# Skip term D·u moved from TensorE to VectorE, paired x-projections, and earlier copies of turned exponentials in a Mamba–attention–feed-forward kernel

## The chip, the core and the metric

The kernel runs on one core of one Trainium2 chip. The metric is device time in microseconds (us). Three runs before the change gave 4987.43, 4989.93 and 4991.37 us; the median is 4989.93 us. One further execution was recorded by the hardware profiler: it took 4984.05 us, of which the program's span in the trace is 4982.3 us, so 1.75 us lie around the span.

The engines are named as in the profile: PE is TensorE's matmul side and PEld its weight loads, DVE is VectorE, ACT is ScalarE, POOL is GpSimd, SP is SyncE, which here only issues transfers. Each engine takes its instructions in one order that is fixed when the program is built.

## What is computed

Eight images of 384 channels and 32x32 pixels (1024 tokens) go through two layers, all in fp32. The first is a convolution beside a bidirectional selective scan (Mamba); the second is causal self-attention with six heads of 64 and a group-quantised feed-forward net, both with residuals. Cut to what the change touches:

```python
# mamba, called forward and on the flipped sequence; the two are added
x_dbl = einsum('blc,ec->ble', u, x_proj_w)              # 24 + 16 + 16 rows
dt, Bm, Cm = split(x_dbl, ...)
delta = softplus(einsum('blr,dr->bld', dt, dt_proj_w) + dt_proj_b)
h = exp(delta * A) * h + (delta * u) * B                # per step, 16 states
y = sum_n h * C
y = (y + u * D_param) * silu(z)                         # the skip term D u
# attention
attn = softmax(where(causal, q @ k.T, -inf)); out = attn @ v
```

## The kernel before, in words

Channels lie on partitions: 384 channels are three groups `c` of 128, and 1024 tokens are two halves `h` of 512, so that nearly every tile is 128x512 fp32, which is also one PSUM bank.

**Stages.** `before_scan` (L307) prepares one image: norm, input projection, causal convolution in both directions `d`, gates, the x-projection to delta, B and C (`project`, L484), and `delta` (L511). The scan is cut into units: one image, one channel group, one of four parts (direction and half, in the order `PARTS`), and two of the 16 states. A unit goes through `slot` (its steps are spread over consecutive slots): loads, `s_first` (POOL: delta·u times B, L588), `s_scan` (ACT: exp into a `da` bank, L601; DVE: the scan, L606; POOL: times C, L612), `s_sum` (PE: eight transposing matmuls add the unit into the `y` bank, L620; at the end of a run y is copied out by ACT at L636 or added by DVE at L641), and `s_gate` (L643), which runs once per image, channel group and half, 48 times in all. `attention` (L676) follows image by image, and `feed_forward` (L970) for the first five images.

**Order of work.** `run` and the timed list at the end of the kernel lay the scan slots of later images beside attention, feed-forward and preparation of others. That is only the order in which instructions are traced. The framework's scheduler then fixes each engine's own order from a priority that follows the traced order and from its own estimate of when operands are ready. `tc.high_priority(offset=n)` moves what is traced inside it forward by n in that priority. `pin` (L73) keeps an instruction behind the one traced just before it on its engine.

**Buffers.** PSUM has eight banks: y 1, da 2, s 2, pt 2, av 1. A scan unit's `g` tile has six buffers. The banks of tag `pt` are shared by the transposes of attention, by the row factors `f`, by parts of `before_scan`, and by `s_gate`.

**s_gate.** The tile `us` holds u of both directions added, `sz` the gate silu(z). Before the change PE put D·u into a `pt` bank with one matmul against a diagonal matrix `diagd` (L656; built at L181 to L183), added eight transposes of the two `yt` tiles on top (L661), and DVE multiplied the gate by the bank (L670). A matmul of fp32 that isn't a transpose appears as two instructions in the profile, so these 48 are 96 there.

**project.** For each image, channel group and half one bank `xp` is filled by two matmuls of 64 columns, one for each direction, on partitions 0 to 63 and 64 to 127 (L487). ACT or DVE then reads the bank.

**turned and weigh.** In attention, `scores` (L774) leaves exponentials `pr` in SBUF (DVE L802, ACT L812). `turned` (L858) transposes blocks of them on PE into a `pt` bank (L864), and ACT copies the bank to SBUF as `ptn` (L866, 576 copies; two buffers for each head of a pair). `weigh` (L869) multiplies the values by `ptn` (L877), one block behind. `at_once(second)` is a local helper in `attention`: it wraps the second matmul of a pair in `tc.high_priority(offset=HURRY)` with HURRY = 400, and is used at L788 and L877 together with `pin`.

Of the kernel before, what the change touches and what calls it, by code (L numbers as in the profile page):

```python
# [12 lines left out]
ALU = mybir.AluOpType  # L13
# [41 lines left out]
def kernel(  # L55
# [49 lines left out]
    def half(h):  # L105
        return slice(h * HB, (h + 1) * HB)
# [71 lines left out]
    amat = ctile("amat", [P, NC, NS])  # L178
    nc.scalar.activation(amat, vec[:, :, V_ALOG : V_ALOG + NS], AF.Exp)
    nc.vector.tensor_scalar(amat, amat, -1.0, None, ALU.mult)  # L180
    diagd = ctile("diagd", [P, NC, P])  # L181
    for c in range(NC):
        nc.vector.tensor_scalar(diagd[:, c, :], ident, vec[:, c, V_D : V_D + 1], None, ALU.mult)  # L183
    rssm = ctile("rssm", [P, 1])
    nc.vector.tensor_tensor(rssm, sc[:, 0:1], sc[:, 1:2], ALU.mult)
    rsh = ctile("rsh", [P, 1])
# [9 lines left out]
    def binarize(src, dst, nk, nout, per, name, emit):  # L196

        gs = nout // GROUPS
        st = {}

        def part(w, k, n):
            return w[k * P : (k + n) * P, :].rearrange("(k p) e -> p k e", p=P)

        def view(k, n):
            t = btile(f"{name}_{k}")
            v = t.rearrange("p c l -> p (c l)")[:, : n * nout].rearrange("p (k e) -> p k e", k=n)
            nc.scalar.dma_start(out=v, in_=part(src, k, n))
            return v

        starts = list(range(0, nk, per))  # L210

        @emit
        def _():
            st["mps"] = bank(f"mps_{name}", "av")

        for k in starts:

            @emit
            def _(k=k, n=min(per, nk - k)):
                v = view(k, n)  # L220
                sums = small.tile([P, GROUPS], F32, name=f"sums_{name}_{k}", tag="bsums", bufs=1)
                for g in range(GROUPS):
                    nc.vector.tensor_reduce(
                        sums[:, g : g + 1], v[:, :, g * gs : (g + 1) * gs], AX.XY, ALU.add
                    )
                nc.tensor.matmul(
                    out=st["mps"][:, :GROUPS],
                    lhsT=onesc,
                    rhs=sums,
                    start=(k == 0),  # L230
                    stop=(k == starts[-1]),
                )

        @emit
        def _():
            st["mean"] = small.tile([P, GROUPS], F32, name=f"mean_{name}", tag="bmean", bufs=1)
            nc.vector.tensor_scalar(
                st["mean"], st["mps"][:, :GROUPS], C / (gs * nk * P), None, ALU.mult
            )

        for k in starts:

            @emit
            def _(k=k, n=min(per, nk - k)):
                v = view(k, n)
                for g in range(GROUPS):
                    z = v[:, :, g * gs : (g + 1) * gs]
                    nc.vector.tensor_scalar(z, z, st["mean"][:, g : g + 1], None, ALU.subtract)
                t = btile(f"sg_{name}_{k}")
                sg = t.rearrange("p c l -> p (c l)")[:, : n * nout].rearrange("p (k e) -> p k e", k=n)  # L250
                z, sg = v[:, :, : GROUPS * gs], sg[:, :, : GROUPS * gs]
                nc.scalar.activation(sg, z, AF.Sign)
                nc.vector.tensor_tensor(sg, sg, z, ALU.subtract)
                nc.vector.tensor_tensor(z, z, sg, ALU.add)
                nc.vector.memset(v[:, :, GROUPS * gs :], 0.0)
                nc.scalar.dma_start(out=part(dst, k, n), in_=v)


    def mean_of(c_of, name):
# [47 lines left out]
    def before_scan(b, tags, emit, later=None, diags=None):  # L307
# [107 lines left out]
        for c in range(NC):  # L415

            @emit
            def _(c=c):
                st["up", c] = mtile(f"up_{b}_{c}")
                for d in range(2):  # L420
                    st["u", d, c] = mtile(f"u{d}_{b}_{c}")
                if c + 1 < NC:
                    weights_of(c + 1)

            for i, to in enumerate((emit, emit if later is None else later)):
                for h in range(NH):
                    to(lambda c=c, i=i, h=h: in_proj(c, i, h), 2.6)
            for d in range(2):
                for h in range(NH):
                    emit(lambda c=c, d=d, h=h: conv(c, d, h), 3.0)  # L430

            def silus(ts):
                for t in ts:
                    pin(nc.scalar.activation(t, t, AF.Silu))

            def sum_of_us(c=c):
                usum = mtile(f"us_{b}_{c}")
                nc.vector.tensor_tensor(usum, st["u", 0, c], st["u", 1, c], ALU.add)
                spill((b, "us", c), usum, f"sus_{b}_{c}")
                for d in range(2):  # L440
                    spill((b, "u", d, c), st["u", d, c], f"su_{d}_{b}_{c}")


            def gates(c=c, silus=silus, sum_of_us=sum_of_us):
                st["xc"] = mtile(f"xc_{b}_{c}")
                load(st["xc"], x[b, chunk(c), :])
                accs = [local(c, h) for h in range(NH)]
                with tc.high_priority(offset=60):
                    us = [st["u", 0, c], st["u", 1, c]] if later is None else []
                    silus(us + [st["z", c]])  # L450
                    for h in range(NH):
                        pin(
                            nc.scalar.activation(
                                accs[h], accs[h], AF.Tanh, scale=0.5, bias=dwbh[:, c : c + 1]
                            )
                        )
                    pin(nc.scalar.preload_act_table_set(LOG_EXP))
                for h in range(NH):
                    acc, xc = accs[h], st["xc"][:, half(h)]
                    nc.vector.scalar_tensor_tensor(  # L460
                        acc, acc, 1.0, st["xn"][:, c, half(h)], ALU.add, ALU.mult
                    )
                    nc.vector.scalar_tensor_tensor(xc, acc, rsh, xc, ALU.mult, ALU.add)  # L463
                spill((b, "t", c), st["xc"], f"st_{b}_{c}")
                spill((b, "z", c), st["z", c], f"sz_{b}_{c}")
                if later is None:
                    sum_of_us()

            def gates_of_us(c=c, silus=silus, sum_of_us=sum_of_us):
                with tc.high_priority(offset=60):  # L470
                    silus([st["u", 0, c], st["u", 1, c]])
                    pin(nc.scalar.preload_act_table_set(LOG_EXP))
                sum_of_us()

            if later is None:
                emit(gates, 14.0)
            else:
                emit(gates_of_us, 4.0)
                later(gates, 10.0)


            for h in range(NH):

                def project(c=c, h=h):  # L484
                    xp = bank_of(f"xp_{b}_{c}_{h}")
                    for d in range(2):
                        nc.tensor.matmul(  # L487
                            out=xp[d * DW : (d + 1) * DW, :],
                            lhsT=wx[:, c, :],
                            rhs=st["u", d, c][:, half(h)],  # L490
                            start=True,
                            stop=True,
                        )
                    xd = st["xd"][:, half(h)]
                    if c == 0:
                        nc.scalar.activation(xd, xp, AF.Identity, bias=onerow)
                    else:
                        nc.vector.tensor_tensor(xd, xd, xp, ALU.add)

                emit(project)  # L500
# [142 lines left out]
    def s_gate(u):  # L643
# [6 lines left out]
        for what in ("us", "z"):  # L650
# [2 lines left out]
            both.append(t)  # L653
        us, sz = both
        tp = bank(f"yb_{u.name}", "pt")
        nc.tensor.matmul(  # L656
            out=tp, lhsT=diagd[:, c, :], rhs=us, start=True, stop=False, skip_group_check=True
        )
        for yt in yts:
            for i in range(QT):  # L660
                nc.tensor.matmul(  # L661
# [1 line left out]
                    lhsT=yt[:, i, :],  # L663
                    rhs=ident,
                    is_transpose=True,
                    start=False,
                    stop=(yt is yts[-1] and i == QT - 1),
                    skip_group_check=True,
                )
        nc.vector.tensor_tensor(sz, sz, tp, ALU.mult)  # L670
        t = dram.tile([P, HB], F32, name=f"sgy_{u.name}", tag=f"sp_gy_{c}_{h}")
        nc.sync.dma_start(out=t, in_=sz)
# [3 lines left out]
    def attention(b, emit_ffn, emit):  # L676
# [79 lines left out]
            st["o"] = btile(f"o_{b}")  # L756

        def at_once(second):  # L760
            return tc.high_priority(offset=HURRY) if second else nullcontext()

        def rows_of(e):
            return slice(e * HD, (e + 1) * HD)
# [57 lines left out]
        def weighted_values(c, g, steps):  # L822
# [35 lines left out]
            def turned(j):  # L858
                cols = slice(max(j - g * QT, 0) * P, HB)
                for e in range(2):  # L860
# [2 lines left out]
                        pr = st["pr", c, g, i, j // QT]  # L863
                        nc.tensor.transpose(pt[:, chunk(i)], pr[:, e, chunk(j % QT)], ident)  # L864
                    ptn = ptp.tile([P, HB], F32, name=f"ptn_{b}_{c}_{g}_{j}_{e}", tag=f"ptn{e}")
                    nc.scalar.copy(ptn[:, cols], pt[:, cols])  # L866
                    st["ptn", j, e] = ptn

            def weigh(j):  # L869
# [354 lines left out]
```

## Time and profile before

| quantity | value |
|---|---|
| median of three runs | 4989.93 us |
| profiled execution | 4984.05 us |
| its span | 4982.3 us |
| mean granted TensorE clock | 0.884 of full speed |
| HBM traffic | 527.33 MB read, 165.68 MB written, 139 GB/s |
| transfers on SP's queue | 40.9% of the 16 DMA engines' time |
| scan transposes L620 | 6144 instructions, 949.1 us busy on PE |
| state multiplications L588 and L612 | 768 each, 1840.4 and 1822.1 us busy on POOL |
| scans L606 | 1536, 906.5 + 953.3 us busy on DVE |
| exponentials L601 | 1536, 1057.3 us busy on ACT |

A line of the profile's groups reads: source line, engine, operation, what is written from what, shape, count; then busy time and the mean duration of one in ns; then how long the engine had been idle just before such instructions, and what ended that idle time. Busy time is a union: two matmuls that overlap count once. Matmul ends are modelled in the trace, so busy PE time is not work at peak rate.

The scan ends at about 4680 us, and image 7's attention follows it without scan work beside it.

### The profile page before, as it was taken

Reading aid. Unit: us, or ns where it says so; the run is one execution under the profiler, and the core shown is the slowest. Engines: PE = TensorE matmul, PEld = TensorE weight load, DVE = VectorE, ACT = ScalarE, POOL = GpSimd, SP = SyncE. Lnnn points to the kernel's source line nnn. Section 1 sums busy time; section 2 is a strip of 40 time slices with the busy share of each in tenths; the row PEclk is TensorE's granted clock in tenths of the full one; section 3 lists DMA queues with packets and bytes.
Section 4 is the critical chain, followed back from the end, with each engine's and each line's share of the span. In section 5 each row is a group of like instructions: output and inputs, shape, how many; then the busy total and the mean of one; then the engine's idle time right before and its main releaser. Section 6 shows DMA issues by size and latency. Waiting matters only on the chain. (4 is left out here: it accounts for less than half of the span.)

```text
span 4982.3 us, 50788 instructions
## 1 busy us (share of the span) xinstructions
PE 4058.8 (81%) x16458; PEld 2192.3 (44%) x16458; DVE 3607.8 (72%) x4771; ACT 2668.1 (54%) x4858; POOL 3696.0 (74%) x1944
## 2 busy tenths in 40 slices
PE   3687786988888888788787888887888988888989
PEld 1243343544444444345443444443454544444444
DVE  6887988677886768786778867687867676676623
ACT  4575655565554655545656446555456365464425
POOL 0578687997768986779876788867789888888800
PEclk7788797899989899888998888998899988999999
DMA  6554646324463335463334633334533333334210
GB/s 230 204 185 151 200 164 229 114 93 130 140 220 120 112 116 168 136 200 123 100 125 147 210 111 129 112 130 157 193 130 116 113 110 124 131 102 137 93 58 26
DMA packets 365010, 696.36 MB, mean 140 GB/s; under 512 B 30104, under 2 KB 88904, under 8 KB 364744
## 3 DMA queue, kind: packets, MB, share of 16 engines
q1 hardware_dynamic: 355232, 676.97, 40.9%
q10 hardware_dynamic: 9512, 16.15, 0.9%
q8 instruction: 130, 2.13, 0.2%
q14 instruction: 136, 1.11, 0.1%
HBM read 527.33 MB, written 165.68 MB: 139 GB/s over the span
## 5 line engine op out<-in xcount | busy, mean ns | idle before, releaser
L588 POOL TENSOR_TENSOR g<-ud,bc 128x1024 f32<-128x1024 f32 x768 | 1840.4, 2396 | 579.8 <-PE y L620 452.0
L612 POOL TENSOR_TENSOR g<-g,bc 128x1024 f32<-128x1024 f32 x768 | 1822.1, 2373 | 251.7 <-DVE g L606 157.8
L601 ACT ACTIVATE da<-dl,amat 128x512 f32<-128x512 f32 x1536 | 1057.3, 691 | 1532.5 <-DVE g L606 1498.3
L606 DVE TENSOR_TENSOR_SCAN g<-da,g 128x512 f32<-128x512 f32 x768 | 906.5, 1210 | 475.4 <-POOL g L588 457.2
L606 DVE TENSOR_TENSOR_SCAN g<-da,carry,g 128x512 f32<-128x512 f32 x768 | 953.3, 1271 | 384.2 <-POOL g L588 354.1
L620 PE MATMUL y<-ident,g 128*128 128x128 f32 x6144 | 949.1, 303 | 266.7 <-POOL g L612 123.1
L620 PEld LDWEIGHTS y<-ident,g 128*128 128x128 f32 x6144 | 789.3, 156 | 714.4 <-issue 418.9
L788 PE MATMUL s<-k,q 64*128 64x512 f32 (+3 forms) x1152 | 384.5, 600 | 128.9 <-DVE nm L802 110.5
L802 DVE CUSTOM_DVE_ANT_0 pr<-s,cmask 128x512 f32<-128x512 f32 (+3 forms) x576 | 299.5, 545 | 178.2 <-PE s L788 177.9
L812 ACT ACTIVATE pr<-pr,nm 128x512 f32<-128x512 f32 (+3 forms) x576 | 348.9, 607 | 123.5 <-DVE nm L802 121.6
L864 PE MATMUL pt<-ident,pr 128*128 128x128 f32 x1728 | 304.0, 309 | 93.6 <-ACT ptn L866 55.1
L995 PE MATMUL hp<-t,w 128*128 128x512 f32 x720 | 334.9, 610 | 28.7 <-DMA w<-w1s 18.3
L1039 PE MATMUL yp<-h,w 128*128 128x512 f32 x720 | 332.6, 620 | 15.3 <-DMA w<-w2s 12.1
L864 PEld LDWEIGHTS pt<-ident,pr 128*128 128x128 f32 x1728 | 217.7, 155 | 245.0 <-ACT ptn L866 110.3
L877 PE MATMUL av<-ptn,v 128*64 128x512 f32 (+3 forms) x1152 | 273.1, 555 | 50.4 <-ACT ptn L866 33.9
L341 PE MATMUL in<-xn,win 128*128 128x512 f32 x576 | 282.3, 636 | 32.3 <-DVE xc L463 8.6
L866 ACT COPY ptn<-pt 128x512 f32<-128x512 f32 (+3 forms) x576 | 255.3, 472 | 49.8 <-PE pt L864 48.4
L727 PE MATMUL qp<-t,wqk 128*128 128x512 f32 x576 | 266.4, 613 | 11.7 <-DVE t L302 9.1
L400 DVE SCALAR_TENSOR_TENSOR loc<-xn,vec,loc 128x496 f32<-128x496 f32 (+3 forms) x384 | 259.9, 721 | 19.5 <-ACT loc L389 18.2
L788 PEld LDWEIGHTS s<-k,q 64*128 64x128 f32 x1152 | 132.3, 206 | 261.2 <-DVE nm L802 179.6
L611 POOL COPY carry<-g 128x2 f32<-128x2 f32 x384 | 87.0, 226 | 205.9 <-DVE g L606 205.8
L1039 PEld LDWEIGHTS yp<-h,w 128*128 128x128 f32 x720 | 142.0, 201 | 189.1 <-issue 169.4
(153 smaller groups left out, 4722.4 us busy)
## 6 DMA issues: line engine op xcount, KB each, us to landing
bc<-rows SPq DMA_DIRECT2D x512, 512.0 KB, 4.1
dl<-sdl SPq DMA_DIRECT2D x160, 256.0 KB, 2.9
ud<-sud SPq DMA_DIRECT2D x160, 256.0 KB, 2.7
t<-st SPq DMA_DIRECT2D x63, 512.0 KB, 5.1
su<-u SPq DMA_DIRECT2D x48, 512.0 KB, 3.4
du<-su SPq DMA_DIRECT2D x96, 256.0 KB, 3.8
sdl<-du SPq DMA_DIRECT2D x96, 256.0 KB, 2.8
sud<-du SPq DMA_DIRECT2D x96, 256.0 KB, 2.3
```

The costliest lines, as they stand in the source:

```text
L341: nc.tensor.matmul(out=mp, lhsT=st["win", c][:, k, i, :], rhs=st["xn"][:, k, half(h)], start=(k == 0), stop=(k == NC - 1),)
L588: pin(nc.gpsimd.tensor_tensor(g, ud, sst["bc", 0, u.b, u.part, u.n], ALU.mult))
L601: nc.scalar.activation(da, sst["dl", u.b, u.c, u.part], AF.Exp, scale=amat[:, u.c, n : n + 1])
L606: nc.vector.tensor_tensor_scan(gi[:, ::step], da[:, ::step], gi[:, ::step], first, ALU.mult, ALU.add)
L612: pin(nc.gpsimd.tensor_tensor(g, g, sst["bc", 1, u.b, u.part, u.n], ALU.mult))
L620: nc.tensor.matmul(out=y[:, j, :], lhsT=g[:, i, chunk(j)], rhs=ident, is_transpose=True, start=(u.opens and i == 0 and j == 0), stop=(u.cl ...
L788: mm = nc.tensor.matmul(out=ss[e][:, : k1 - k0], lhsT=st["q"][rows_of(e), c, chunk(qi)], rhs=st["k"][rows_of(e), c, k0:k1], start=True, st ...
L802: nc.vector.tensor_tensor_reduce(out=x, in0=ss[e][:, :w], in1=mask, scale=-1.0, scalar=-MASKED, op0=ALU.add, op1=ALU.min, accum_out=m,)
L812: nc.scalar.activation(x, x, AF.Exp, bias=m, scale=-1.0, accum_out=rs[:, i, e, kb : kb + 1])
L864: nc.tensor.transpose(pt[:, chunk(i)], pr[:, e, chunk(j % QT)], ident)
L995: nc.tensor.matmul(out=hp, lhsT=st["w1"][:, c, chunk(m % 2)], rhs=st["xn"][:, c, half(h)], start=(c == 0), stop=(c == NC - 1),)
L1039: nc.tensor.matmul(out=yp, lhsT=st["w2", k // 6][:, k % 6, :], rhs=st["h", k // NC][:, k % NC, half(h)], start=(k == 0), stop=(k == NF - 1),)
```

## The change

Three edits, and one that only moves a helper.

1. The diagonal matrices and the diagonal matmul of `s_gate` are gone. The first transposing matmul of each gate opens the bank. DVE then adds D·u to the bank in place with one `scalar_tensor_tensor` (u times a per-partition scalar, plus the bank), ahead of the multiplication by the gate.
2. The second direction's x-projection is traced at priority offset 400 and pinned behind the first's.
3. The copies `ptn` are traced at priority offset 60.

`at_once` moves from `attention` to the kernel's outer scope, so that `project` can use it too.

```diff
-    diagd = ctile("diagd", [P, NC, P])
-    for c in range(NC):
-        nc.vector.tensor_scalar(diagd[:, c, :], ident, vec[:, c, V_D : V_D + 1], None, ALU.mult)
...
+    def at_once(second):
+
+        return tc.high_priority(offset=HURRY) if second else nullcontext()
...
                     for d in range(2):
-                        nc.tensor.matmul(
-                            out=xp[d * DW : (d + 1) * DW, :],
-                            lhsT=wx[:, c, :],
-                            rhs=st["u", d, c][:, half(h)],
-                            start=True,
-                            stop=True,
-                        )
+                        with at_once(d == 1):
+                            mm = nc.tensor.matmul(
+                                out=xp[d * DW : (d + 1) * DW, :],
+                                lhsT=wx[:, c, :],
+                                rhs=st["u", d, c][:, half(h)],
+                                start=True,
+                                stop=True,
+                            )
+                        if d == 1:
+                            pin(mm)
...
         tp = bank(f"yb_{u.name}", "pt")
-        nc.tensor.matmul(
-            out=tp, lhsT=diagd[:, c, :], rhs=us, start=True, stop=False, skip_group_check=True
-        )
         for yt in yts:
             for i in range(QT):
                 nc.tensor.matmul(
...
                     is_transpose=True,
-                    start=False,
+                    start=(yt is yts[0] and i == 0),
                     stop=(yt is yts[-1] and i == QT - 1),
                     skip_group_check=True,
                 )
+        nc.vector.scalar_tensor_tensor(tp, us, vec[:, c, V_D : V_D + 1], tp, ALU.mult, ALU.add)
         nc.vector.tensor_tensor(sz, sz, tp, ALU.mult)
...
-                    nc.scalar.copy(ptn[:, cols], pt[:, cols])
+                    with tc.high_priority(offset=60):
+                        nc.scalar.copy(ptn[:, cols], pt[:, cols])
```

More of the change, by code (lines that the diff above doesn't have):

```diff
@@ L756, in _ @@
             st["o"] = btile(f"o_{b}")
-        def at_once(second):
-            return tc.high_priority(offset=HURRY) if second else nullcontext()
         def rows_of(e):
```

## The prediction, made before the changed kernel had run

> **What bounds the kernel now.** I read the page's first two parts first, then the list of waits, then the rows of the lines that the diff touches.
>
> ```profile
> PE 4058.8 (81%) x16458; PEld 2192.3 (44%) x16458; DVE 3607.8 (72%) x4771; ACT 2668.1 (54%) x4858; POOL 3696.0 (74%) x1944
> PE   3687786988888888788787888887888988888989
> POOL 0578687997768986779876788867789888888800
> PEclk7788797899989899888998888998899988999999
> ```
>
> No engine is full. PE is nearest, at eight tenths in most slices and alone in the last two, and POOL stands beside it from the third slice to the 38th. The clock row matters as much: where PE has gaps it is granted less than full speed. So PE's idle time is the place to look: 4982.3 - 4058.8 = 923.5 us. The waits of all engines, longest first (engine and line, releaser, total us, times, longest):
>
> ```profile
> ACT da L601 <- DVE g L606: 1498.3, 1071, 14.7
> DVE g L606 <- POOL g L588: 811.3, 448, 10.2
> POOL g L588 <- PE y L620: 452.0, 202, 14.1
> ...
> PE y L620 <- POOL g L612: 123.1, 51, 10.5
> ```
>
> Read backwards, this is a ring: exponentials wait for scans, scans for POOL, POOL for PE to free a g buffer (452.0 us), and PE for POOL (123.1 us). POOL waits for PE over three times as long as PE for POOL. I take PE's ordered queue, its work and its small stalls, as what mostly sets the pace, with POOL close behind. The waits of PE alone:
>
> ```profile
> PE s L788 <- DVE nm L802: 110.5, 89, 3.4
> PE y L620 <- ACT yt L636: 77.0, 22, 11.9
> PE y L620 <- DVE yt L641: 56.2, 17, 7.5
> PE pt L864 <- ACT ptn L866: 55.1, 43, 3.8
> ...
> PE av L877 <- ACT ptn L866: 33.9, 16, 4.0
> ...
> PE pt L864 <- DVE zh L670: 22.5, 11, 3.5
> ...
> PE f L849 <- ACT ptn L866: 14.3, 11, 3.5
> ```
>
> The copies ptn end 55.1 + 33.9 + 14.3 us here and 1.8 at L656, 105.1 us of PE's idle time, in 73 waits; the gate's product zh ends 22.5 us of it. The groups' rows of the matmuls that go or are paired:
>
> ```profile
> L656 PE MATMUL yb<-ush,diagd 128*128 128x512 f32 x96 | 60.0, 712 | 3.7 <-ACT ptn L866 1.8 <-DVE du L527 1.1 <-ACT u L379 0.5
> L487 PE MATMUL xp<-u,wx 128*64 128x512 f32 x192 | 78.2, 704 | 60.5 <-ACT u L434 49.9 <-ACT u L379 9.8 <-DVE zh L670 0.9
> ```
>
> **What the Trainium skill says.** "TensorE: Matmul & The Clock Gate", Part 1, says that the array runs at full or half rate by how busy it has been of late. The trace agrees: L656 takes 592 ns at least and 1222 at most, and PEclk averages 0.884. So a PE with less to do may be granted less. The same page (section on the array's architecture) says that ACT and DVE keep strict FIFO order; so a copy moved forward can also hold up what stands behind it. Nothing in this trace contradicts that. "TensorEngine Tiling (Array Packing)", Key Properties, says that tiles run in parallel, and 64 columns make two tiles. The trace shows it at L487, on PE's timeline with start, duration and count: the four instructions of two directions take 1.08 us, those of one direction at both halves 1.93.
>
> ```profile
> 1242.73 1.08 PE L487 MATMUL xp<-u,wx 128*64 128x512 f32 x4
> ...
> 471.76 1.93 PE L487 MATMUL xp<-u,wx 128*64 128x512 f32 x4
> ```
>
> "VectorE: DVE Perf Modes", the tier table, puts any two-tensor operation that reads PSUM at one element a cycle. The row below has the same form as the new addition (SBUF times a per-partition scalar, plus PSUM, into PSUM), so its duration is used.
>
> ```profile
> L369 DVE SCALAR_TENSOR_TENSOR u<-up,vec,u 128x512 f32<-128x512 f32 x90 | 66.0, 745 | 3.4 <-ACT u L358 3.3
> ```
>
> **The change, part by part.** Beside the trace I compared the order of instructions in the two built programs, engine by engine. POOL's is identical, 1949 of 1949. On PE 144 instructions give way to 96 (the 48 diagonal matmuls go, the 96 projections have a new line), on DVE 48 additions come and three diagonal builds go. SP issues the same 1724, most in the same order. ACT's order changes most.
>
> *Diagonal matmul.* One matmul is two instructions. In a dense stream one takes 0.43 us (24 of L1039 in 10.30 us, in the chain of waits), so one matmul 0.86 us, as PE's starts around L656 show where the clock is full. 48 x 0.86 = 41 us at full speed, 41 / 0.884 = 47 us as granted; 60.0 us is the row's busy time, with the pipeline's filling, and is the upper bound. What reaches the end depends on PE's next stall. Following PE's records from each of the 48 to the next gap over 0.3 us, the gap is ended by something other than a scan sum in 33 cases (attention's own transposes, scores, projections: these come earlier too when PE does) and in 15 by L620, where PE waits for POOL or for the y copy and simply waits longer. 47 x 33/48 = 32 us. Bounds: 15 (a third) to 60.
>
> *Copies ptn.* Matching each copy with its transposes by order, copies start on average 1.1 us after their last transpose ended (sum 635 us over 576), mostly because ACT is in exponentials pr (L812) or da (L601). In the new order 335 of the 375 displaced copies stand earlier; together they pass 218 pr and 144 da. With L812 at 607 + 188 ns (the row of the accumulator read) and L601 at 691 ns: 218 x 0.795 + 144 x 0.691 = 273 us over 576 copies, 0.47 us each. 73 stalls x 0.47 = 34 us of PE idle time. Half of it will meet the next stall (scores waiting for nm, 110.5 us, are in the same stretches): 17 us gained. The exponentials that are passed are covered: an exp da takes 0.69 us and a scan 1.21 to 1.27, with two da banks, so ACT has 0.5 us a scan to spare, and DVE waits for da only 42.4 us now (L606's two rows, 27.5 + 14.9). Bounds: -10 (copies that block ACT) to 60 gained.
>
> *Paired projections.* The tie holds nothing back: it brings the second direction forward only once it can run, and the first is issued as before. In the order, 31 of 48 pairs stand side by side before, 33 after; three are won and one is lost. Saved: 2 x (1.93 - 1.08) = 2 us. Bounds 0 to 5.
>
> *The new addition.* 48 x 0.745 = 36 us more on DVE, which is 72% busy, so most of it lies in DVE's idle time. What reaches PE: the pt bank comes free 0.745 us later after the last transpose. PE waited for zh in 14 cases on its list (11 at L864, three elsewhere): 14 x 0.745 = 10 us lost. The bank is opened 0.86 us later, so the hold as a whole isn't longer. Scans queue behind the additions on DVE: the 36 us meet POOL's product L612, which waited 157.8 us for scans; I take a tenth, 3 us. Bounds 3 to 36. What hides the rest is DVE's wait for POOL (811.3 us).
>
> *The rest.* The transfers of us and z wait for the same DVE instructions; one table load of 1.28 us less on ACT, two copies of v on DVE instead of ACT: nothing.
>
> Sum: -32 - 17 - 2 + 13 = -38 us against the profiled execution, 4984.05 - 38 = 4946 us. The median of the runs stands 5.9 us above that execution, so 4989.93 - 38 = 4952 us.
>
> **Rivals.** *A: PE's gain turns into waiting.* Stalls at L620 (123.1 + 77.0 + 56.2 = 256 us) grow by what PE saves while POOL, at 6 to 9 tenths in the later half, sets the pace. For: POOL's row. Against: POOL's 452.0 us behind PE. Then the final stage and a few stretches gain: about a quarter of 51 us less the 13 us of DVE: nothing, 4990 us.
>
> *B: slower. ACT is blocked by the earlier copies.* A copy that stands ahead of da but whose transposes are late holds the queue. ACT already idles 48.4 us for pt before copies (62 times), and about 120 of the 576 copies start within 0.15 us of their transposes, so they have no room to come earlier. If 200 copies hold ACT for 0.47 us, that is 94 us; when over half of that appears in scans waiting for da, 47 + 13 us of loss stand against 32 + 2 us of PE's gain, the copies' own gain being gone: 26 us more, 5016 us. Against: only 144 exponentials da are passed, and ACT is 46% idle.
>
> *C: the copies were the lever.* Nearly all the 105.1 us go, and the denser PE keeps its clock: -32 - 60 - 2 + 10 = -84, 4906 us. For: they are late by 635 us in sum. Against: only 273 us of passing.
>
> **How the numbers follow.** Forecast 0.55 (4920 to 4978), A 0.2, B 0.17, C 0.08. Below 0.2%, 10 us, a difference can't be told from none here. Faster: the forecast, C and 0.07 of A: 0.70. Same: 0.12 of A and 0.01 of B: 0.13. Slower: 0.17, most of B and a rest of A. The range 4905 to 5008 leaves out about half of C's and half of B's chance and the forecast's tails, under 0.2; it is set by the unknown pass-through (15 to 60) and the copies (-10 to 60).
>
> **What would show it.** Right: no L656; PE busy lower by 45 to 60 us; a new DVE row of 48 at about 745 ns; waits of L864, L877 and L849 for ptn down from 103 to about 65 us; L864 waiting for zh up from 22.5 to about 33; POOL's wait for L620 lower. Wrong: L620's waits up by 30 us or more (A); L606 waiting for da well above 42 us, and ACT idle before L866's successor above 100 (B); a mean clock under 0.87 (0.01 of clock is worth 4059 x 0.01 / 0.884 = 46 us).

## The result, and the profile after

The changed kernel took 4952.93 us (median of four runs, 4947.72 to 4958.55) against 4988.68 us before in the same comparison (4981.59 to 4991.37): a ratio of 0.9934, 95% interval 0.9915 to 0.9954, so 23 to 42 us gained. The forecast was 4952 us. The profiled execution fell from 4984.05 to 4952.38 us, by 31.7 us, where 38 were forecast.

The total came out almost to the microsecond, but two of the four terms under it were wrong: the copies brought nothing where a gain was forecast, and the new addition cost less than was forecast. First the changed kernel's page, busy time and some of the rows by slices:

```profile
PE 4007.3 (81%) x16362; PEld 2168.0 (44%) x16362; DVE 3659.0 (74%) x4818; ACT 2669.5 (54%) x4855; POOL 3696.7 (75%) x1944
...
PE   4677786988788788688887888887887988988889
...
POOL 0487787996878986768876699867799888888800
PEclk7787796999989899888898998898899989989999
```

PE has 96 instructions and 51.5 us of busy time less (4058.8 to 4007.3), inside the 45 to 60 foretold. The mean clock hardly moved (0.884 to 0.885). PE's idle time went up from 923.5 to 943.3 us: the span is 31.7 us shorter and PE waits 19.8 us more. These are differences of two single executions. The next view is the changed kernel's list of PE's waits (line, releaser, total us, times, longest):

```profile
PE y L624 <- POOL g L616: 122.2, 61, 7.0
...
PE pt L863 <- ACT ptn L866: 78.5, 52, 4.5
PE dp L522 <- DVE du L531: 67.6, 21, 9.9
PE y L624 <- ACT yt L640: 61.0, 19, 13.1
PE y L624 <- DVE yt L645: 56.0, 18, 10.1
...
PE av L877 <- ACT ptn L866: 35.8, 16, 4.0
...
PE f L848 <- ACT ptn L866: 16.8, 13, 2.7
...
PE pt L863 <- DVE zh L672: 8.6, 12, 1.6
```

Line numbers have moved: L624 was L620, L863 was L864, L848 was L849, L522 was L518, L672 was L670; L592 and L616 of POOL were L588 and L612. Two entries contradict the prediction. The waits for the copies ptn should have gone from 103 to about 65 us over L863, L877 and L848; they are 78.5 + 35.8 + 16.8 = 131 us. The wait for the gate's product zh should have gone from 22.5 to about 33 us; it is 8.6. The largest rise after that of the copies is one that the prediction didn't name: in the preparation of an image PE's matmuls to delta (L522) wait 67.6 us for DVE's product du, after 49.3 before. And in the list over all engines POOL waits less for PE, as it should, 391.9 us after 452.0:

```profile
POOL g L592 <- PE y L624: 391.9, 180, 15.0
...
POOL g L616 <- DVE g L610: 196.1, 19, 28.9
```

The rows of DVE by shape show the addition with the duration that was taken for it, 745 ns, and the product right behind it with no idle time of its own:

```profile
L671 DVE SCALAR_TENSOR_TENSOR yb<-ush,vec,yb 128x512 f32<-128x512 f32 x48 | 35.8, 745 | 36.7 <-PE yb L662 28.5 <-issue 3.4 <-ACT da L605 2.8
L672 DVE TENSOR_TENSOR zh<-zh,yb 128x512 f32<-128x512 f32 x48 | 32.2, 670 | 0.1
```

### The profile page after: what moved, and what is told of

Read it like the earlier page. It is cut to its first block, busy times and chain, and to the rows that moved or that the text cites. A ratio compares the mean times of both kernels' runs of the same rounds, so it can differ in the third digit from the quotient of the medians.

```text
span 4950.6 us, 50616 instructions
## 1 busy us (share of the span) xinstructions
PE 4007.3 (81%) x16362; PEld 2168.0 (44%) x16362; DVE 3659.0 (74%) x4818; ACT 2669.5 (54%) x4855; POOL 3696.7 (75%) x1944
## 5 line engine op out<-in xcount | busy, mean ns | idle before, releaser
L592 POOL TENSOR_TENSOR g<-ud,bc 128x1024 f32<-128x1024 f32 x768 | 1843.2, 2400 | 518.7 <-PE y L624 391.9
L616 POOL TENSOR_TENSOR g<-g,bc 128x1024 f32<-128x1024 f32 x768 | 1821.0, 2371 | 271.1 <-DVE g L610 196.1
L624 PE MATMUL y<-ident,g 128*128 128x128 f32 x6144 | 938.7, 301 | 249.2 <-POOL g L616 122.2
L624 PEld LDWEIGHTS y<-ident,g 128*128 128x128 f32 x6144 | 782.0, 155 | 696.7 <-issue 379.8
L863 PE MATMUL pt<-ident,pr 128*128 128x128 f32 x1728 | 301.9, 307 | 98.1 <-ACT ptn L866 78.5
L863 PEld LDWEIGHTS pt<-ident,pr 128*128 128x128 f32 x1728 | 216.2, 154 | 240.2 <-ACT ptn L866 134.5
L877 PE MATMUL av<-ptn,v 128*64 128x512 f32 (+3 forms) x1152 | 270.8, 551 | 49.7 <-ACT ptn L866 35.8
```

The lines of the kernel that those rows point to most:

```text
L592: pin(nc.gpsimd.tensor_tensor(g, ud, sst["bc", 0, u.b, u.part, u.n], ALU.mult))
L616: pin(nc.gpsimd.tensor_tensor(g, g, sst["bc", 1, u.b, u.part, u.n], ALU.mult))
L624: nc.tensor.matmul(out=y[:, j, :], lhsT=g[:, i, chunk(j)], rhs=ident, is_transpose=True, start=(u.opens and i == 0 and j == 0), stop=(u.cl ...
L877: mm = nc.tensor.matmul(out=av[rows_of(e), cols], lhsT=st["v"][:, j, hd * HD : (hd + 1) * HD], rhs=st["ptn", j, e][:, cols], start=(j % QT ...
```

## The experiments

The kernel before was timed again with each group of runs. Its median was 4983.87 us in the first group, 4995.97 in the second and 4985.77 in the third, so the ratios are compared, and closely only within a group.

### The three edits, each alone, and the first two together

The first run keeps only the move of the skip term.

```diff
 (against the changed kernel: projections and copies as before the change)
-                        with at_once(d == 1):
...
-                    with tc.high_priority(offset=60):
-                        nc.scalar.copy(ptn[:, cols], pt[:, cols])
+                    nc.scalar.copy(ptn[:, cols], pt[:, cols])
```

> Only the first edit: the skip term on DVE, no diagonal matmul; projections and copies as before. Theory P (the prediction's sum: diagonal -32, addition +13, copies -17, pairs -2): 19 us faster than before, about 0.996. Theory D (the whole gain comes from the diagonal matmul; the copies bring nothing, since PE's wait for them rose from 105.1 to 133.2 us in the changed kernel): 32 to 45 us faster, about 0.991 to 0.994, and PE's wait for the gate's product stays under the 22.5 us of before. Theory A (PE's gain turns into waiting at the scan sums): within 10 us of before.

Measured: 4949.48 us, ratio 0.9937 (0.9921 to 0.9953), by the ratio 31 us gained. This edit alone is worth as much as the whole change. PE's wait for zh, all of it at the transposes of attention, fell with it:

```profile
PE pt L860 <- DVE zh L669: 6.8, 10, 1.7
```

The second keeps only the copies' priority, with the diagonal matmul back.

```diff
 (against the kernel before; the moved helper left out)
-                    nc.scalar.copy(ptn[:, cols], pt[:, cols])
+                    with tc.high_priority(offset=60):
+                        nc.scalar.copy(ptn[:, cols], pt[:, cols])
```

> Only the third edit: the turned copies at priority offset 60; diagonal matmul and projections as before. Theory P: 17 us faster, about 0.9966, and PE's waits for the copies fall from 105.1 us to 70 or less. Theory D: 0 to 5 us either way, and these waits don't fall. Rival B (copies that stand ahead of their transposes block ACT): slower by 10 us or more, and ACT's idle time before the copies, 49.8 us before, rises by 20 or more.

Measured: 4991.08 us, ratio 1.0013 (1.0003 to 1.0022), by the ratio some 6 us slower (1 to 11). PE's waits for the copies, from its list of waits:

```profile
PE pt L865 <- ACT ptn L868: 76.7, 51, 4.5
...
PE av L879 <- ACT ptn L868: 34.6, 16, 4.0
...
PE f L850 <- ACT ptn L868: 12.0, 11, 2.4
...
PE yb L660 <- ACT ptn L868: 2.1, 3, 0.7
```

That is 125.4 us, after 105.1 before: the very waits that the priority might have lowered are higher. ACT idled 56.7 us for transposes right before a copy (48.4 before), not 20 us more, so the block of rival B isn't what happened. Matching copies with their transposes by order, the copies did become less late: 564 us in sum, after 635. What ACT did meanwhile shows where that came from. Exponentials pr overlap these delays by 148 us, after 244; exponentials da by 178, after 165. And in both kernels ACT stands idle for over 120 us (122 and 129) with a finished bank behind it, in front of a da; nearly all of ACT's idle time before da (1498.3 of 1532.5 us in the kernel before) ends with a scan. In the order of this kernel copies pass 219 exponentials pr and only 39 da. So the priority takes away delays behind pr and leaves those behind da as they were. The prediction had counted 144 da over all three edits; in the order of the first edit alone, without any priority, copies already pass 97 da against the kernel before. Offsets 400 and 3000 in place of 60 leave the order of copies and exponentials as it is: with each of the three, when all three edits are in, the priority itself passes 48 da. That fits a scheduler that brings a copy forward only to where it believes the transposes done; kernels with these offsets were not timed.

The third keeps only the tie of the projections.

```diff
+                        with at_once(d == 1):
+                            mm = nc.tensor.matmul(
...
+                        if d == 1:
+                            pin(mm)
```

> Only the second edit: the second direction's projection hurried and pinned. 34 pairs of 48 stand side by side in its order, 31 before. Both theories: 0 to 5 us faster, not to be told from none; PE busy at the projections falls from 78.2 us by about 3. If it differs by more than 10 us, the reshuffled order itself, and not the pairs, is worth that much.

Measured: 4985.39 us, ratio 0.9999 (0.9987 to 1.0011). As expected, nothing. This one small reshuffle of the order is worth at most some 6 us either way, by its interval; the 6 us of the copies' priority are no larger than that, and may be of that kind.

The fourth is the changed kernel with the copies as before the change.

> The changed kernel without the third edit: skip term on DVE and tied projections, copies as before. Theory P: 17 us slower than the changed kernel, so 19 to 21 us faster than before (0.996). Theory D: as fast as the changed kernel or faster, 33 to 45 us faster than before (0.991 to 0.9935), with PE's waits for the copies at about 105 us or less.

Measured: 4944.34 us, ratio 0.9934 (0.9916 to 0.9952), the same ratio as with all three edits. This fits theory D: the first edit is the whole gain, as far as these intervals tell.

### What the matmul and the addition cost by themselves

The fifth and sixth run take the kernel with the first edit alone. One leaves the addition out, so that D·u isn't computed at all; the other makes it twice.

```diff
-        nc.vector.scalar_tensor_tensor(tp, us, vec[:, c, V_D : V_D + 1], tp, ALU.mult, ALU.add)
```

> The kernel with the first edit alone, and the DVE addition left out: the skip term D u isn't computed. It tells the cost of the 48 additions. Theory P (13 us of the 36 reach the end): 13 us faster than the kernel with the first edit alone, 0.991 of before. Theory F (the addition is free: PE's wait for the gate's product fell from 22.5 to 6.8 us with it, and DVE has idle time): within 5 us of the first edit alone, 0.9925 to 0.9945 of before.

> The kernel with the first edit alone, with the DVE addition made twice, so that D u enters twice. 48 more DVE instructions of 0.745 us, 36 us of DVE time. Theory P: 13 us slower than the first edit alone, 0.996 of before. Theory F: within 5 us of it, 0.993 to 0.9945 of before.

Measured: without it 4950.03 us, ratio 0.9905 (0.9890 to 0.9920); twice 4954.17 us, 0.9916 (0.9901 to 0.9932). From none to 96 additions the ratio moves by 0.0011, 5 us, which the intervals don't tell from zero. So 48 additions cost about 3 us, and not 13, which would have made 26 between these two runs. With the addition made twice PE's wait for zh at attention's transposes isn't longer:

```profile
PE pt L861 <- DVE zh L670: 4.0, 4, 1.6
```

The seventh run takes the kernel before and makes the diagonal matmul twice, each with half of D.

```diff
-        nc.vector.tensor_scalar(diagd[:, c, :], ident, vec[:, c, V_D : V_D + 1], None, ALU.mult)
+        nc.vector.tensor_scalar(diagd[:, c, :], ident, vec[:, c, V_D : V_D + 1], 0.5, ALU.mult, ALU.mult)
...
         nc.tensor.matmul(
             out=tp, lhsT=diagd[:, c, :], rhs=us, start=True, stop=False, skip_group_check=True
         )
+        nc.tensor.matmul(
+            out=tp, lhsT=diagd[:, c, :], rhs=us, start=False, stop=False, skip_group_check=True
+        )
```

> The kernel before with the diagonal matmul made twice, each with half of D. 48 more matmuls, 41 us at full clock, 47 as granted. It tells the price of such a matmul by itself. Theory P: 32 us slower than before, 1.0064. Theory M (PE's order is the pace almost everywhere, and all of it reaches the end): 40 to 50 us slower, 1.008 to 1.010. Theory A: under 15 us slower. If it is 0 to 15 while removal brought 34, the removal's gain came from elsewhere than PE's time.

Measured: 5029.59 us, ratio 1.0067 (1.0051 to 1.0082), 33 us slower (25 to 41). That is the price of 48 more such matmuls, 0.7 us each at the end of the kernel, beside the prediction's 32 for taking 48 away. The yardstick of this group makes it less sure than the interval says: the kernel before ran 10 to 12 us slower here than in the other two groups, while kernels with the first edit took 4944 to 4956 us in all three. From its page and rows:

```profile
span 5029.6 us, 50983 instructions
...
PE 4085.7 (81%) x16554; PEld 2191.3 (44%) x16554; DVE 3618.6 (72%) x4772; ACT 2670.1 (53%) x4857; POOL 3699.4 (74%) x1944
...
L659 PE MATMUL yb<-ush,diagd 128*128 128x512 f32 x96 | 57.3, 683 | 0.0
```

PE's busy time is 26.9 us above that of the kernel before, and its share of the span is the same 81%. The added row alone is 57.3 us; the rest of PE's work took less time, at a mean clock of 0.889 after 0.884. As an estimate of the work at full speed, busy time times mean clock rises from 3588 to 3632 us, by 44, where the prediction had 41. PE's idle time rose too, by 20.4 us, so the two traces differ by more than the medians.

### Pairs that stand side by side

In the changed kernel 33 of 48 pairs stand together, because the hurried second direction can't hold the first back; with the first edit alone it is 31. Tracing the second direction first, whose operand is ready last, and hurrying the first behind it gives all 48. Skip term and copies are those of the first edit alone.

```diff
 (against the changed kernel; the copies, as before the change, left out)
-                    for d in range(2):
-                        with at_once(d == 1):
+                    for d in (1, 0):
+                        with at_once(d == 0):
...
-                        if d == 1:
+                        if d == 0:
```

> The first edit, copies as before, and the projections traced with the second direction first, whose operand is ready last, and the first direction hurried and pinned behind it: all 48 pairs stand side by side in the order, against 33. 15 more pairs at 0.85 us, 13 us of PE's time. If PE's time is the pace: 9 to 13 us faster than with the first edit alone, 0.991 to 0.992 of before. If the projections mostly stand where PE waits for their operands anyway (it waited 60.5 us there before): within 5 us of the first edit alone.

Measured: 4949.25 us, ratio 0.9904 (0.9888 to 0.9921), but its yardstick had run on another chip. So both ran again side by side:

> The first edit alone once more, on the same chip as the next three, as their yardstick. 0.9905 to 0.9945 of before.

> The first edit with all 48 pairs side by side (second direction traced first), once more beside the first edit alone. PE's busy time at the projections was 22 us lower in its trace (57.7 against 79.7). If freed PE time reaches the end as the diagonal matmul's did (33 of 47 us): 15 us faster than the first edit alone, 0.997 of it. If it only lengthens PE's waits: within 5 us.

Measured: 4952.13 us, 0.9935 (0.9911 to 0.9959), for the first edit alone, and 4950.12 us, 0.9928 (0.9903 to 0.9953), with the pairs: not to be told apart. The row of the projections by shape, first without and then with the pairs:

```profile
L488 PE MATMUL xp<-u,wx 128*64 128x512 f32 x192 | 79.3, 702 | 61.1 <-ACT u L435 50.3 <-ACT u L380 10.8
```

```profile
L489 PE MATMUL xp<-u,wx 128*64 128x512 f32 x192 | 58.4, 722 | 51.6 <-ACT u L435 50.2 <-DVE xc L464 1.3
```

And PE's waits at the scan sums until 850 us, in the same order (L621 and L624 are the same line):

```profile
PE y L621 <- POOL g L613: 63.7, 30, 7.8
...
PE y L621 <- ACT yt L637: 11.5, 3, 6.0
...
PE y L621 <- DVE yt L642: 8.8, 4, 2.6
```

```profile
PE y L624 <- POOL g L616: 78.2, 33, 7.7
...
PE y L624 <- DVE yt L645: 19.6, 6, 5.6
...
PE y L624 <- ACT yt L640: 13.1, 3, 6.3
```

PE's busy time at the projections fell by 21 us, 19 of them until 850 us, and these waits at the scan sums rose by 27 (84.0 to 110.9). Of the 17 pairs that were newly won, 15 lie in this stretch, where images 1 to 3 are prepared beside the first scans. The freed time doesn't bring PE forward: the projections of image 4 begin at 1246.4 us in the first trace and at 1244.8 in the second. After 850 us these waits are much the same in both (164.2 and 167.0 us). Waiting at the scan sums isn't the whole account, though. All of PE's busy time until 850 us fell by 10.6 us only, and the mean clock over the ten executions with all pairs was 0.881, after 0.884 over the eleven of the first edit alone. So a part of what the pairs save may go into slower matmuls; the runs don't separate the two.

### Copies on another engine

The eleventh run gives half of the copies to DVE, on top of the first edit.

```diff
-                    nc.scalar.copy(ptn[:, cols], pt[:, cols])
+                    (nc.scalar.copy if e == 0 else nc.vector.tensor_copy)(ptn[:, cols], pt[:, cols])
```

> The first edit alone, with the turned copies of every pair's second head made by DVE instead of ACT, 288 of 576. In the traces finished transposes wait while ACT is idle in front of an exponential da that itself waits for a scan, and priority doesn't change that. Theory Q (ACT's queue is what holds the copies): PE's waits for copies by ACT fall by a third or more from 111 us; if DVE's queue takes it no worse, 10 to 25 us faster than the first edit alone. Theory R (DVE's queue holds them as long, behind scans that wait for POOL, and 288 copies add about 150 us to DVE): 0 to 30 us slower, with PE waits for copies by DVE of 50 us or more.

Measured: 4952.88 us, ratio 0.9936 (0.9916 to 0.9956), the same as the first edit alone.

```profile
PE pt L860 <- DVE ptn L862: 46.8, 41, 3.9
...
PE pt L860 <- ACT ptn L862: 39.6, 29, 2.8
...
PE av L873 <- DVE ptn L862: 25.0, 13, 3.5
```

With the smaller entries (DVE at L845 and L659 5.8 us, ACT at L845 1.3) PE waits 40.9 us for copies by ACT, after 115.6 beside it, and 77.6 for copies by DVE: 118.5 in all. With half of the copies ACT's queue holds PE for about a third of the time, as theory Q has it, but the gain that Q had isn't there. DVE's queue holds PE for over 50 us, as R has it, and the 158 us of copies on DVE cost nothing that is seen at the end, the lower edge of R's range. That PE waits for copies as long as before, 118.5 after 115.6 us, leaves open what shorter waits would be worth.

The last run repeats the changed kernel.

> The changed kernel itself once more, beside the first edit alone on the same chip. If the copies' priority costs what it cost alone (7 us, 1.0013) and the tie nothing: 2 to 10 us slower than the first edit alone, 1.0005 to 1.002 of it. Theory P: 19 us faster than it.

Measured: 4956.17 us, ratio 0.9943 (0.9923 to 0.9963), 4 us above the first edit alone on the same chip. That is in the direction of the 6 us that the copies' priority cost alone, though these two intervals overlap. Waits for the copies were 138.3 us here, so their rise stands in all three traces with the priority (125.4, 133.2 and 138.3).

No version beat the changed kernel by more than the measurement resolves. The first edit alone is as fast, as far as this tells, and is the simpler kernel.

## Why the prediction was right, and where it was wrong

**The diagonal matmul: right in size.** Forecast 32 us; doubling it cost 33 (25 to 41), and the first edit alone gained 31. The work, 41 us at full speed, is borne out by the 44 us of the doubled matmul. That the stalls' count (33 of 48) is what cuts the 47 granted us down is not shown by itself: no run changes it, and PE's idle time doesn't show the 15 us that should have been absorbed: with the matmul doubled it rose by 20.4 us instead of falling, and in three traces without it (the changed kernel, and the first edit alone twice) it moved by +19.8, -8.4 and +4.2.

**The paired projections: right.** Forecast 2 us; alone 0.9999. That the tie can't hold the first direction back was read from the order of instructions. What the prediction didn't see is that even 17 more true pairs bring nothing that can be measured, as most stand where PE waits for POOL. That is rival A, in the main true for one stage and not for the kernel.

**The copies: wrong, in sign.** The step "73 stalls x 0.47 = 34 us" failed. The advance under it, 273 us in sum, was mis-sized: in the run with this edit alone lateness fell by 71 us. It counted every exponential passed as time won, though finished banks went on standing behind da, and it took the 144 da of the full comparison for the work of this edit, which passes 39 when alone. And the link from lateness to PE's waits failed: they rose by 20 us, and the time by 6. Why PE's waits rose when the copies were less late is not settled. PE's own order moved too (in its trace 173 of attention's 1728 transposes stand earlier in it and 20 later), so PE may come to a bank sooner than the copy does; that was argued from the order, not tried.

**The new addition: wrong in size.** Forecast 13 us lost, measured about 3. The failing term is "14 x 0.745 = 10": all of PE's waits for zh fell instead, from 27.9 us to 6.8 to 8.7 in the traces of the first edit alone and of the changed kernel. The prediction's own sentence that the hold of the bank isn't longer was right: from the last transpose to the end of zh the time rose from 4.5 to 5.6 us on average, but the whole hold, from its first PE instruction, went from 8.6 to 8.0, as the diagonal matmul had opened the bank 2.25 us ahead of the first transpose. The hold isn't what sets the waits, though. With the addition made twice it is 10.0 us, with none 6.3, and PE's waits for zh are 10.4 and 6.4 us. What the waits go with is the diagonal matmul: they sum to 22.5 to 27.9 us in the four traces of kernels that have it, and to 6.4 to 11.0 in the ten of kernels without it. Why is open. The term of 3 us through the scans isn't shown either: POOL's wait for scans at L616 rose by 38 us in the changed kernel, but by 29 in the run without any addition.

Together the measured parts make -33 + 3 + 6 + 0 = -24 us, beside -36 by the medians (interval 23 to 42) and -30 in the repetition (18 to 38). They agree within the intervals. So the exact hit is partly luck: an error of 23 us at the copies stands against one of 10 at the addition, and the 13 that are left lie within the noise. The fall of PE's busy time inside the forecast's 45 to 60 us is in part luck as well: the two executions of the first edit alone lie 22 and 48 us below the kernel before.

**The rivals.** B lost: scans waited 34.5 us for da in the changed kernel (23.9 + 10.6), less than the 42.4 before. Where the copies' priority alone ran slower, ACT's idle time before copies had risen from 48.4 to 56.7 us only. C lost with the copies. A lost for the whole and won, in the main, for the projections.

## What to carry to other kernels

Where no engine is full, price removed work by following the engine from each removed instruction to its next stall, and ask whether what ends that stall moves along: here about 0.7 of the matmul's time as granted reached the end (33 of 47 us), while of 21 us freed at the projections nothing measurable did. Before a copy is given priority, look at what its engine does while the copy is ready, and whether that is what the new order passes; here the priority left the delays in front of da at the head of ACT's queue as they were. And a wait list doesn't say that each wait will grow with its releaser: 14 waits for zh were priced at one addition each, and they went with the matmul that was removed, not with the additions.

## What the runs showed of the hardware

PE's idle time differs less between the versions than its busy time: it lies between 915 and 948 us in fourteen traces, while busy times reach from 3996 to 4086 and spans from 4938 to 5030 us. And busy time differs between executions of one kernel. The kernel with the first edit alone shows it: span and busy time in two executions of the same program,

```profile
span 4952.0 us, 50642 instructions
...
PE 4036.9 (82%) x16362; PEld 2179.9 (44%) x16362; DVE 3645.3 (74%) x4818; ACT 2667.0 (54%) x4855; POOL 3695.2 (75%) x1944
```

```profile
span 4938.1 us, 50642 instructions
...
PE 4010.4 (81%) x16362; PEld 2168.1 (44%) x16362; DVE 3645.5 (74%) x4818; ACT 2667.2 (54%) x4855; POOL 3695.9 (75%) x1944
```

DVE, ACT and POOL agree within 1 us, and PE differs by 26.5 us of busy time at mean clocks of 0.880 and 0.886; busy time times clock is 3552 and 3553 us, the same work. The span differs by 13.9 us, as idle time went the other way. In the eleven executions of the kernel before that went with the last group, the time falls as the clock rises, along one line: from 5004.56 us at 0.882 to 4971.93 at 0.890, correlation -0.97, 3.8 us for each 0.001 of clock. In the 12 executions of the second group the correlation is -0.79, and in the 35 of the first weaker, -0.58, with 1.8 us for each 0.001. The Trainium skill, "TensorE: Matmul & The Clock Gate", Part 1, says that the windows which decide the clock run freely and don't start with the kernel; that could make the same program be granted slightly different clocks. The traces agree with the effect, 0.880 and 0.886 for one program, but no run here shows the windows, so the cause stays open. A change of 0.1% in this kernel is therefore seen only over many executions: the copies alone, at 1.0013, took 21, against 35 of the kernel before.
